# Expert slots filled from both ends, and unscaled products for two sequences, in a two-layer network on one Trainium2 core

## The chip, the cores and the metric

The kernel runs on one core of one Trainium2 chip. The core has TensorE (PE, matmuls; its weight loads are shown as PEld), VectorE (DVE), ScalarE (ACT), GpSimd (POOL, which also issues the indirect DMAs) and SyncE (SP, which issues most other DMAs). The metric is the device time of one execution in microseconds (us). A profiled execution has a span (first to last instruction) and a time of its own that is slightly longer.

## What is computed

The input is `x`, 32 sequences of 256 tokens with 256 features, and a few conditions for each sequence. Cut to its last lines, the reference is

```python
x = x + L0_attn(L0_cond(x, cond_512))             # 16 heads, two softmax attentions
x = x + L0_ffn(L0_cond2(x, cond_512))             # attention, then a mixture of experts
x = x + L1_attn(L1_cond(x, cond_512))             # kernel features of normed q and k
x = x + L1_ffn(L1_cond2(x, ids, ..., cond_64))    # conditioned norms, then butterflies
```

Two pieces matter here. The mixture of experts works on all T = 8192 tokens at once:

```python
top1 = argmax(logits); top2 = argmax(logits without top1)     # 8 experts
loc1 = cumsum(m1) - 1                     # place of a token among those that chose the expert first
loc2 = cumsum(m2) - 1 + m1.sum(0)         # second choices stand behind all first choices
m1 = m1 * (loc1 < C); m2 = m2 * (loc2 < C)                    # C = T / 4 = 2048 places
h = relu(buf[e] @ w1[e] + b1[e]);  y = (h @ w2[e] + b2[e]) * 0.8
out = t1 * y[top1, s1] + t2 * y[top2, s2]                     # t1, t2: gates, normed to sum 1
```

Which tokens an expert keeps depends on `loc` and C. In which order the kept ones are worked on does not enter the result.

The last attention of layer 1 divides q and k by their norms over the whole batch, `q / norm(q)`, `k / norm(k)`, two scalars that are known only when all sequences are done. Then it forms `exp` of a linear function of both: per sequence `exp(yT @ (rn_q * Wq' + rn_k * Wk') + bias)`, where `rn_q` and `rn_k` are the reciprocals of these norms and `Wq'`, `Wk'` are weights prepared earlier.

## The kernel before

The work stands in generator functions that yield the engine and an assumed cost of each step. `side_by_side` merges them, when the program is built, into one order for each engine, by those costs and by "join" marks; each engine then works through its list in order and waits on semaphores. A pause is written `yield None, x`, and a turn object such as `lanes_b` limits how many parts run at once. Changing one part's steps or costs can therefore move instructions of others.

There are four stages.

1. The 32 sequences go through layer 0's attentions, up to about 1583 us. The normed rows that the experts read are stored to DRAM in `h2buf`. When the first 28 sequences are done, their routing is computed beside the other work (`routed_early`): `choices_of` finds both choices, `places_of` counts (`cnt`, `cntb`) and finds places by products with a triangle (`loc`, L569 to L584), `tokens_of` turns the places into a list of tokens by products of one-hot tiles (`tps`, L626). The last 4 sequences make LATE = 8 of the NT = 64 tiles of 128 tokens.
2. Behind a branch (L1440: a second, exact pass over the sequences, which these inputs do not take) comes the routing of the late tiles, `routing` (L1503 to L1525). `ends` (L1527) finds per expert where first choices end; for each expert, first choices fill the slots from the front and second choices from the back, so the number of tokens of each kind must be known first. The late token list is added to the early one (`both` L1514), the two sides are joined (`to` L1517, L1518) and give `tok` (L1520), the token of every slot. `slots` and `gates` (L1552, L1568) compute rows and gates; the gates are transposed (L1612), copied (L1615) and stored to `gbuf` in DRAM (L1618).
3. The experts: 8 experts of CAP = 2048 slots in blocks of CBLK = 512, so 4 blocks for each. `expert_block` (L1675) gathers 4 x 128 rows by `tok` on POOL's queue (L1686), transposes them on PE (L1700) and copies them with ACT (L1703, `ehT`). The first layer is 16 matmul instructions in 8 banks (`bh` L1740), followed by ACT (`hid` L1727), the second layer 32 instructions (`by` L1757), and DVE adds the bias (`ysb` L1763) and multiplies by the gate of the slot (`gslot` L1772). POOL gathers these gates from `gbuf` (L1633, `slot_gates`) and adds the rows to the tokens in DRAM with a scatter (L1643, `add_to_tokens`). A scatter adds to memory, so each waits for the landing of the one before. `load_expert` (L1659) loads w1, w2 and b2 of an expert on SP's queue; for the second expert it waits for a small POOL memset (`behind_gathers`, L1657) behind the first gathers. Each fp32 matmul instruction shows as two records in the trace.
   Beside the experts, DVE multiplies the butterflies of the last feed-forward into a dense matrix (`butterflies` L1809, `butterfly_stage` L1786, with the loads `w_eff` and `bfw`), and shares its buffers with the experts' tiles.
4. `answer` (L1889) finishes the experts' rows of each sequence. `norms` (L2174) sums the squares (`qs`, L2184), and takes the factors `rn` on POOL (L2191), then scales and adds the weights (`mixed`, L2197, L2198). `norm_rows` (L2200) makes the row of biases `aphr` (L2208, L2212) and a scalar `phs`. `answer_out` (L2261), 32 times, is the last phase: the values and the mixed product (L317, by `project`), `exp`, the gathers of norm tables (L2227, on POOL), statistics and their power (L261, L267), modulated norms (L2246, L2248), their transposes (L297) and products (L2353), and the two dense products (L2410, L2424).

PSUM banks and SBUF buffers come from rings named "mm", "sh" and "big": `get` takes the next buffer, `back` returns it, and an instruction that writes a reused buffer waits for its former readers.

Of the kernel before, what the change touches and what calls it, by code (L numbers as in the profile page):

```python
# [14 lines left out]
F = mybir.dt.float32  # L15
# [7 lines left out]
P = 128  # L23
# [195 lines left out]
def network(ctx: ExitStack, tc: tile.TileContext, a: dict, out: bass.AP):  # L219
# [304 lines left out]
    early = cst.tile([P, 2, 2 * NHI], F, name="early")  # L524
# [35 lines left out]
    def places_of(a, b):  # L560
# [3 lines left out]
        wide = [(min(b, (n + 1) * SLAB) - n * SLAB) * NE for n in range(n1)]  # L564
        cps = yield from get("mm", "cnt", [P, 2, NSB])
# [6 lines left out]
        for n in range(n0, n1):  # L572
            yield DVE, 0.15
            nc.vector.tensor_copy(cntb[: wide[n], :, n], cps[: wide[n], :, n])
        yield back("mm")
        step = 2 if 2 * W * NE <= 512 else 1
        for k0 in range(0, 2, step):
# [3 lines left out]
            for i in range(step):  # L581
                nc.tensor.matmul(loc[:, i, :], utb, mbs[:, k0 + i, a * NE : b * NE], start=True, stop=False)
                for n in range(n1):
                    nc.tensor.matmul(  # L584
                        loc[:, i, :], cntb[: wide[n], k0 + i, n : n + 1].to_broadcast([wide[n], P]),
                        before[: wide[n], n, a * NE : b * NE], start=False, stop=(n == n1 - 1),
                    )
# [10 lines left out]
    def tokens_of(a, b, wide, into):  # L598
# [11 lines left out]
        for k, (op, at) in enumerate(((ALU.add, NE * CAP - 1), (ALU.subtract, (NE + 1) * CAP))):  # L610
# [8 lines left out]
        tps = yield from get("mm", "tps", [P, 2, 2 * NHI])  # L619
# [3 lines left out]
        def product(ol, oh, k, t, w):  # L623
            yield PE, 0.135 * w
            for i in range(w):
                nc.tensor.matmul(  # L626
                    tps[:, k, :], ol[:, i // 2, :, i % 2], oh[:, i // 2, :, :, i % 2].rearrange("p a h -> p (a h)"),
                    start=(t + i == 0), stop=(t + i == W - 1),
                )
# [3 lines left out]
        def by_place(ol, oh, o1, k, t, w, before):  # L633
            yield ACT, 0.15 + 0.125 * w
            nc.scalar.activation(oh[:, :, 1, :, :], o1, AF.Copy, scale=prow)
            yield back("sh")
            if before is not None:
# [26 lines left out]
    def routed_early(sequences):  # L664
# [8 lines left out]
        nc.vector.tensor_copy(early, got[0])  # L673
        yield back("mm")
# [803 lines left out]
    wphi, aphi = waq["aq"], abq["aq"]  # L1478
# [22 lines left out]
    cc = wD.tile([P, 2, NE], F, name="cc")  # L1501

    def routing():  # L1503
# [6 lines left out]
        both = yield from get("sh", "both", [P, 2, 2, NHI])  # L1510
        to = wD.tile([P, 2, NHI], F, name="to")
        yield "join", counted
        yield DVE, 0.75
        nc.vector.tensor_add(both.rearrange("p k a h -> p k (a h)"), got[0], early)  # L1514
        yield back("mm")
        yield DVE2, 1.0
        nc.vector.tensor_tensor(to, both[:, 1], late.unsqueeze(1).to_broadcast([P, 2, NHI]), ALU.mult)  # L1517
        nc.vector.tensor_add(to, to, both[:, 0])  # L1518
        yield DVE, 0.3
        nc.vector.scalar_tensor_tensor(tok, to[:, 0], float(P), to[:, 1], ALU.mult, ALU.add)  # L1520
        yield back("sh")
# [5 lines left out]
    def ends():  # L1527

        ps = yield from get("mm", "mm", [P, 2, NE])
        yield PE, 0.5  # L1530
        for k in range(2):
            for n in range(NSB):
                w = min(SLAB, NT - n * SLAB) * NE
                nc.tensor.matmul(
                    ps[:, k, :], cntb[:w, k, n : n + 1].to_broadcast([w, P]), e8b[:w],
                    start=(n == 0), stop=(n == NSB - 1),
                )
# [3 lines left out]
        from_ = wD.tile([P, NE], F, name="from_")  # L1541
        E3 = [P, NE, CAP // P]
        yield DVE, 1.0
        nc.vector.tensor_scalar(from_, cc[:, 1, :], -1.0, float(CAP), ALU.mult, ALU.add)
        for o, v in ((late, cc[:, 0, :]), (used, from_)):
            nc.vector.tensor_tensor(
                o.rearrange("p (e h) -> p e h", e=NE), place.unsqueeze(1).to_broadcast(E3),
                v.unsqueeze(2).to_broadcast(E3), ALU.is_ge,
            )
        nc.vector.scalar_tensor_tensor(used, late, 0.0, used, ALU.is_equal, ALU.max)  # L1550
# [17 lines left out]
    def gates():  # L1568
# [3 lines left out]
        sm_, den = column("sm_"), column("den")  # L1572
        yield DVE2, 0.7
# [9 lines left out]
        for k in range(2):  # L1583
            m = mbs[:, k, :].rearrange("p (t e) -> p t e", e=NE)
            s_ = nths[:, k, :]
            if k == 1:

                s_ = column("s1")
                yield DVE2, 0.7
# [995 lines left out]
```

## Time and profile before

| | |
|---|---|
| runs | 3622.98, 3613.11, 3611.27 us; median 3613.11 |
| profiled execution | 3614.65 us |
| its span | 3612.9 us |
| mean granted clock of PE | 0.978 |
| PE busy | 3433.1 us (95%) |
| sequences | 0 to about 1583 us |
| branch left | 1586.3 us (first work behind it: DVE 1586.27, SP 1586.30) |
| late routing, PE partly idle | 1586.3 to 1600.4 us |
| experts, PE full | 1610 to 2523 us |
| answers and norms | 2523 to 2683 us |
| last phase | 2683 to 3613 us |

The page lists for each engine its busy time and share of the span, then the span in slices, the DMA queues, the chain of work that ended last, and the groups of instructions by line. A row of the timeline gives the start and duration in us, the engine, the line, the operation, out<-in with shapes, a count, and in brackets how long the engine was idle before and what ended that. A row of windows gives for a stretch its length and the busy time of each engine in it (with the count of instructions), then the clock that PE was granted (1.00 is full speed), the mean busy share of the DMA engines, and GB/s. Busy PE is not PE at its peak: a matmul at half clock counts as busy too.

### The profile page before, as it was taken

Reading aid. Unit: us, or ns where it says so; the run is one execution under the profiler, and the core shown is the slowest. Engines: PE = TensorE matmul, PEld = TensorE weight load, DVE = VectorE, ACT = ScalarE, POOL = GpSimd, SP = SyncE. Lnnn points to the kernel's source line nnn. Section 1 sums busy time; section 2 is a strip of 40 time slices with the busy share of each in tenths; the row PEclk is TensorE's granted clock in tenths of the full one; section 3 lists DMA queues with packets and bytes.
Section 4 is the critical chain, followed back from the end, with each engine's and each line's share of the span. In section 5 each row is a group of like instructions: output and inputs, shape, how many; then the busy total and the mean of one; then the engine's idle time right before and its main releaser. Section 6 shows DMA issues by size and latency. Waiting matters only on the chain. (4 is left out here: it accounts for less than half of the span.)

```text
span 3612.9 us, 55000 instructions
## 1 busy us (share of the span) xinstructions
PE 3433.1 (95%) x21397; PEld 2522.7 (70%) x21397; DVE 2295.8 (64%) x3817; ACT 1780.4 (49%) x2751; POOL 1733.7 (48%) x1388
## 2 busy tenths in 40 slices
PE   6798999999999999959999999999989999999999
PEld 5465566666666666636666666667878888888888
DVE  7988889988888884647665620101347666666664
ACT  2677778888787877732222222223334333343332
POOL 3655756566466555226545555553123334344331
PEclk9899999999999999979999999999999999999999
DMA  3344434444444442133334333332441323233221
GB/s 86 66 95 96 92 91 105 104 97 103 94 100 99 100 96 71 56 121 107 89 91 109 106 73 52 64 54 47 161 143 39 123 97 113 80 124 101 97 97 44
DMA packets 192239, 332.67 MB, mean 92 GB/s; under 512 B 55041, under 2 KB 116673, under 8 KB 181730
## 3 DMA queue, kind: packets, MB, share of 16 engines
q0 software_dynamic: 56768, 163.68, 20.1%
q1 hardware_dynamic: 135058, 164.86, 14.6%
q8 instruction: 171, 2.80, 0.3%
q14 instruction: 98, 0.80, 0.1%
q10 hardware_dynamic: 144, 0.52, 0.0%
HBM read 204.03 MB, written 52.58 MB: 71 GB/s over the span
## 5 line engine op out<-in xcount | busy, mean ns | idle before, releaser
L1090 ACT ACTIVATE pt<-sc 128x2048 f32<-128x2048 f32 x256 | 481.5, 1881 | 122.8 <-PE sc L1081 116.1
L1727 ACT ACTIVATE hid<-bh,cols 128x512 f32<-128x512 f32 (+1 forms) x261 | 175.9, 674 | 604.5 <-PE bh L1740 603.4
L1757 PE MATMUL by<-w,hid 128*128 128x256 f32 x2048 | 452.2, 379 | 0.0
L1740 PE MATMUL bh<-ehT,w 128*128 128x512 f32 (+1 forms) x1056 | 450.8, 581 | 0.1
L1757 PEld LDWEIGHTS by<-w,hid 128*128 128x128 f32 x2048 | 387.4, 190 | 65.3 <-issue 15.8
L267 POOL TENSOR_TENSOR n<-n,negh 128x32 f32<-128x32 f32 x64 | 366.9, 5733 | 5.3
L1740 PEld LDWEIGHTS bh<-ehT,w 128*128 128x128 f32 x1056 | 200.6, 191 | 216.4 <-issue 207.5
L261 POOL TENSOR_SCALAR rstd<-mv 128x2 f32<-128x2 f32 x160 | 65.9, 412 | 583.0 <-DVE mv L367 563.1
L1643 POOL DMA_INDIRECT rrows<-ysb,row x128 | 222.6, 1739 | 253.3 <-DMA rrows<-ysb,row 138.4
L1763 DVE TENSOR_TENSOR ysb<-by,b 128x512 f32<-128x512 f32 (+1 forms) x66 | 44.5, 674 | 469.6 <-PE by L1757 431.8
L1081 PE MATMUL sc<-qT,kT 32*128 32x256 f32 x4096 | 298.7, 406 | 14.4 <-ACT pt L1090 12.6
L1063 PE MATMUL av<-pt,vaug 128*32 128x256 f32 x4096 | 276.0, 387 | 7.0 <-ACT pt L1090 6.1
L893 DVE TENSOR_TENSOR hprod<-hex,kk 128x2048 f32<-128x2048 f32 x120 | 275.9, 2320 | 0.0
L1081 PEld LDWEIGHTS sc<-qT,kT 32*128 32x128 f32 x4096 | 188.2, 187 | 102.8 <-issue 52.1
L2410 PE MATMUL dh<-zT,w_eff 128*128 128x256 f32 x1024 | 235.4, 379 | 0.6 <-DVE zT L2386 0.6
L2424 PE MATMUL do<-w_con,gT 128*128 128x256 f32 x1024 | 231.1, 379 | 0.0
L2424 PEld LDWEIGHTS do<-w_con,gT 128*128 128x128 f32 x1024 | 192.5, 190 | 24.9
L2410 PEld LDWEIGHTS dh<-zT,w_eff 128*128 128x128 f32 x1024 | 189.8, 190 | 24.3 <-DVE zT L2386 1.0
L1686 POOL DMA_INDIRECT xg<-h2buf,tok x128 | 139.9, 1093 | 137.4 <-issue 31.8
L1063 PEld LDWEIGHTS av<-pt,vaug 128*32 128x32 f32 x4096 | 107.5, 110 | 135.5 <-issue 67.6
L2400 ACT ACTIVATE gT<-dh,b_eff 128x256 f32<-128x256 f32 x256 | 106.2, 472 | 141.4 <-PE dh L2410 138.8
L267 POOL TENSOR_TENSOR rstd<-rstd,negh 128x2 f32<-128x2 f32 x160 | 164.1, 1025 | 13.3
(622 smaller groups left out, 7023.9 us busy)
## 6 DMA issues: line engine op xcount, KB each, us to landing
hprod<-hprod POOLq DMA_DIRECT2D x60, 1024.0 KB, 7.8
oT<-rden SPq DMA_DIRECT2D x64, 256.0 KB
w<-in_w SPq DMA_DIRECT2D x16, 1024.0 KB
x<-rrows SPq DMA_DIRECT2D x64, 256.0 KB
bfw<-in_upw SPq DMA_DIRECT2D x10, 1024.0 KB
bfw<-in_dnw SPq DMA_DIRECT2D x10, 1024.0 KB
xT<-in_xT SPq DMA_DIRECT2D x32, 256.0 KB
avT<-avT SPq DMA_DIRECT2D x256, 32.0 KB
```

Of the source, the lines that this page charges most:

```text
L267: nc.gpsimd.tensor_tensor(o, o, negh[:p].to_broadcast([p, n]), ALU.pow)
L893: nc.vector.tensor_tensor(pr.rearrange("p j (h d) -> p j h d", d=DH), weights(t, j0, 8)[:, 0].unsqueeze(3).to_broadcast([P, 8, H, DH]), wi ...
L1063: nc.tensor.matmul(av[32 * i : 32 * i + 32, c % 2, :], va[:, kc, HO * (4 * c + i) : HO * (4 * c + i) + 32], pt[:, i, kc, :], start=(kc == ...
L1081: nc.tensor.matmul(sc[:, i, kc, :], kT[r, m, kc * P : (kc + 1) * P], qT[r, e, m, :], start=True, stop=nm is None,)
L1090: nc.scalar.activation(pt, sc, AF.Exp, scale=1.0 / math.sqrt(DH))
L1643: nc.gpsimd.indirect_dma_start(rrows[:, :], bass.IndirectOffsetOnAxis(ap=row[:, j0 + t : j0 + t + 1], axis=0), y[:, t, :], None, compute_o ...
L1686: nc.gpsimd.indirect_dma_start(xg[t], None, h2buf[:, :], bass.IndirectOffsetOnAxis(ap=tok[:, j : j + 1], axis=0))
L1727: nc.scalar.activation(o, ps, AF.Relu, bias=bcol)
L1740: nc.tensor.matmul(ps, w["w1"][:, c, f * P : (f + 1) * P], hT[c][:, c0 : c0 + wide * P], start=(c == 0), stop=(c == 1))
L1757: nc.tensor.matmul(ps[:, t, :], hid[f // 4][:, f % 4, (t0 + t) * P : (t0 + t + 1) * P], w["w2"][:, f, :], start=(f == 0), stop=(f == 7),)
L2410: nc.tensor.matmul(ps[:, g, :], w_eff[:, c, f * P : (f + 1) * P], zT[:, c, :], start=(c == 0), stop=(c == 1))
L2424: nc.tensor.matmul(ps[:, t, :], gT[:, f, t * P : (t + 1) * P], w_con[:, f, :], start=(f == 0), stop=(f == 7))
```

## The change

There are two parts.

**Slots.** Early tokens (the first 28 sequences), first and second choices alike, now fill an expert's slots from the front, and late tokens from the back. So the early list is final when `routed_early` ends, and a new tile `etok` holds it. Blocks 0 and 1 of each expert (`ahead`, the first 1024 of 2048 slots) gather by `etok` and don't join the late routing; blocks 2 and 3 gather by `tok` as before. To place second choices behind first ones within the early tokens, `places_of` multiplies the counts of the first choice into the places of the second; the late tiles have counts of their own (`lcnt`). Both choices go into one accumulation `tps` of half the width. `ends` finds four borders per expert rather than one, `gates` adds the other side's counts to the places. The load of the first expert is split: w1 at once, w2 behind the gathers of block 0. The parts are listed in another order, with the butterflies behind the routing, and there are some pauses (8.0, 5.0, 30.0, 4.0).

```diff
+    etok = cst.tile([P, NHI], I32, name="etok")
...
-                for n in range(n1):
+                for n in range(n0, n1):
+                    w = wide[n]
+                    if k0 + i == 1:
+                        nc.tensor.matmul(
+                            loc[:, i, :].rearrange("p (t e) -> p t e", e=NE), counts[:w, 0, n : n + 1].to_broadcast([w, P]),
+                            e8b[:w].unsqueeze(1).to_broadcast([w, W, NE]), start=False, stop=False,
+                        )
...
-        for k, (op, at) in enumerate(((ALU.add, NE * CAP - 1), (ALU.subtract, (NE + 1) * CAP))):
+        op, at = (ALU.add, NE * CAP - 1) if a == 0 else (ALU.subtract, (NE + 1) * CAP)
+        for k in range(2):
...
-                    start=(t + i == 0), stop=(t + i == W - 1),
+                    start=(k == 0 and t + i == 0), stop=(k == 1 and t + i == W - 1),
...
+        nc.vector.scalar_tensor_tensor(etok, early[:, 0], float(P), early[:, 1], ALU.mult, ALU.add)
...
-        nc.vector.tensor_add(both.rearrange("p k a h -> p k (a h)"), got[0], early)
+        nc.vector.tensor_tensor(to, got[0], of_late.unsqueeze(1).to_broadcast([P, 2, NHI]), ALU.mult)
...
-        nc.vector.tensor_tensor(to, both[:, 1], late.unsqueeze(1).to_broadcast([P, 2, NHI]), ALU.mult)
-        nc.vector.tensor_add(to, to, both[:, 0])
+        nc.vector.tensor_tensor(early, early, of_early.unsqueeze(1).to_broadcast([P, 2, NHI]), ALU.mult)
+        nc.vector.tensor_add(to, to, early)
...
+        yield None, 5.0
         ps = yield from get("mm", "mm", [P, P])
         yield PE, 0.2
         nc.tensor.transpose(ps[: 2 * NT, :], g12.rearrange("p k t -> p (k t)"), ident)
...
         nc.sync.dma_start(w["w1"], a["w1"][e].rearrange("(c p) f -> p c f", p=P))
+        if e == 0:
+            yield DMA, 3.0
+            yield None, 2.0
+            yield first_half
+            yield from behind_gathers(w["w2"][:, 0, 0:1])
...
-        yield "join", routed
+        ahead = blk < (CAP - LATE * P) // CBLK
+        if not ahead:
+            yield "join", routed
...
-                xg[t], None, h2buf[:, :], bass.IndirectOffsetOnAxis(ap=tok[:, j : j + 1], axis=0)
+                xg[t], None, h2buf[:, :], bass.IndirectOffsetOnAxis(ap=(etok if ahead else tok)[:, j : j + 1], axis=0)
...
-    matrices = Part(butterflies([]))
+    matrices = Part(butterflies([routed]))
...
-            [routed, loads[0], blocks[0], loads[1], matrices, *blocks[1:], weights_part, *loads[2:], table_part, *first_parts, square_part, norm_part, rows_part]
+            [loads[0], routed, blocks[0], blocks[1], loads[1], matrices, *blocks[2:], weights_part, *loads[2:], table_part, *first_parts, square_part, brows, norm_part, rows_part, scaled_part]
```

**Last phase.** For the first two sequences, `answer_out` multiplies by `Wq'` and `Wk'` unscaled, before the norms are known, and leaves both products in PSUM. When `rn` is there, two DVE operations scale and add them. The biases become rows earlier (`bias_rows`, from unscaled ones) and are scaled with `rn`. The weights for the other 30 sequences are scaled later (`scaled_weights`), into the same tile.

```diff
+        if b < 2:
+            yield "join", phi_there
+            for n in ("aq", "ak"):
+                ps = yield from get("mm", "mm", [P, 2, D])
+                two.append(ps)
+                yield PE, 1.75
+                project(ps, yT, waq[n])
+            yield unscaled[b]
+            yield back("sh")
...
+        if b < 2:
+            rn = norm["rn"]
+            yield DVE, 1.5
+            nc.vector.scalar_tensor_tensor(ph, two[1], rn[:, 1:2], rows, ALU.mult, ALU.add)
+            nc.vector.scalar_tensor_tensor(ph, two[0], rn[:, 0:1], ph, ALU.mult, ALU.add)
+            yield back("mm")
+        else:
+            yield "join", scaled_part
...
         norm.update(tot=tot, rn=rn)
-        yield DVE, 1.2
-        mixed(waq, rn)
+        yield "join", brows
+        yield DVE, 0.7
+        nc.vector.tensor_scalar_mul(aphr, brow["aq"], rn[:, 0:1])
+        nc.vector.scalar_tensor_tensor(aphr, brow["ak"], rn[:, 1:2], aphr, ALU.mult, ALU.add)
+
+    def bias_rows():
+
+        yield "join", phi_there
+        yield "join", first_parts[4]
+        for n in ("aq", "ak"):
+            ps = yield from get("mm", "mm", TS)
+            yield PE, 0.5
+            for c in range(2):
+                nc.tensor.matmul(
+                    ps[:, 0, c * P : (c + 1) * P], abq[n][:, c : c + 1].to_broadcast([P, P]), ident, start=True, stop=True
+                )
+            yield ACT, 0.4
+            nc.scalar.copy(brow[n], ps[:, 0, :])
+            yield back("mm")
```

## The prediction

> **What bounds the kernel now.** I read the page first, then the windows where its PE digits are not 9, then the timelines of those windows, and the chain of waits for the second.
>
> ```profile
> span 3612.9 us, 55000 instructions
> PE 3433.1 (95%) x21397; PEld 2522.7 (70%) x21397; DVE 2295.8 (64%) x3817; ACT 1780.4 (49%) x2751; POOL 1733.7 (48%) x1388
> ```
>
> PE is idle for only 180 us in all. Nothing that shortens DVE, ACT or POOL work beside a busy PE can matter; what counts is where PE stands still. The windows show two such places near the diff:
>
> ```profile
> core 0: us, PE busy (x) PEld busy (x) DVE busy (x) ACT busy (x) POOL busy (x), PEclk, DMA share, GB/s
> 1580.00:1590.00 10.00, 2.69 (x16) 2.17 (x14) 2.48 (x12) 1.19 (x3) 0.00 (x0) 0.50 0.33 114
> 1590.00:1600.00 10.00, 4.44 (x34) 2.74 (x31) 7.96 (x25) 2.30 (x2) 0.00 (x0) 0.50 0.45 144
> 1600.00:1610.00 10.00, 2.43 (x8) 1.48 (x8) 9.50 (x24) 1.06 (x2) 6.29 (x8) 0.50 0.32 88
> 1610.00:1620.00 10.00, 9.92 (x22) 4.28 (x21) 1.62 (x6) 3.87 (x6) 7.57 (x8) 0.85 1.03 354
> 2690.00:2700.00 10.00, 6.79 (x29) 5.37 (x28) 8.24 (x21) 2.05 (x4) 7.87 (x8) 0.92 0.80 264
> 2700.00:2710.00 10.00, 2.24 (x9) 1.49 (x9) 8.04 (x17) 1.17 (x2) 3.19 (x5) 0.59 0.22 82
> ```
>
> From 1610 on PE is full until 2523 (eight experts, 913 us, 114 us each). The first gap is the routing of the last sequences' tokens ahead of the first expert; the second is the start of the last phase. What ends the first gap:
>
> ```profile
> 1600.14 0.29 DVE L1520 SCALAR_TENSOR_TENSOR tok<-to 128x128 int32<-128x128 f32 x1
> 1602.15 1.16 POOL L1686 DMA_INDIRECT xg<-h2buf,tok  x1 [23.53 <-DVE rf L1562]
> 1608.99 1.33 PE L1700 MATMUL mm<-ident,xg 128*128 128x128 f32 x5 [0.74 <-DMA xg<-h2buf,tok]
> 1610.40 2.07 PE L1740 MATMUL bh<-ehT,w 128*128 128x512 f32 x2
> ```
>
> POOL has waited 23.53 us for the token list; from its first gather to the first expert product pass 1610.40 − 1602.15 = 8.25 us.
>
> **Expert slots, the start.** The list `etok` is finished before the branch at L1440, and blocks 0 and 1 no longer wait for late routing. POOL can gather when the branch is left; the other engines' first work behind it is at 1586.27 (DVE) and 1586.30 (SP), so I take 1586.4. Plus 8.25, the first product is at 1594.65 rather than 1610.40: **−15.75 us**. The late one-hot and place matmuls ahead of it stay, and take 2 us from 1588.21 to 1590.9, before the first gather lands. Both kernels start the experts cold (clock 0.50 until 1613), so no gain is booked for the clock.
>
> Now w1 of expert 0 (1 MB, issued 1586.30) travels beside these gathers; before, they had the queues to themselves. At the 376 GB/s of the window 1610 to 1615 it takes 2.8 us, so the gathers lose between 0 and 2.8; they are small and interleave, so I take **+0.3**. w2 waits behind them, is issued near 1592 and is needed by the first second-layer product, at 1594.65 + 12 first-layer products, the tokens' matmuls and 4 more: about 1612.5. That is cover of some 15 us.
> The Trainium skill ("DMA: Bandwidth & Descriptors", section "Latency and other measured facts") speaks against this step: it gives an HBM access 0.2 us on average and 2 us under high load, so gathers beside a load would land up to 1.8 us later; by that the sum below would be worse by 1.5 us. No row here shows gathers of these rows landing beside a load that PE waited for.
>
> **What moves into the busy stretch.** The 16 token products (L626) stood in the gap (3.57 us at clock 0.50); now they run between first-layer products. At full clock half: **+1.8**. Gates, ends and slots grow by some twenty small DVE operations (0.15 to 0.7 us by the rows of L1514 to L1607), all beside a PE that has work; uncovered they would be about 6 us.
>
> **The backlog this leaves.** The gates are late relative to the experts. Token list at 1611.7 (second group of tokens' products at about 1610.5, then three DVE steps); gates 11.3 us as in the rows from 1600.35 to 1611.7, plus 2 for their added operations: 1625. The transposed gates are copied on DVE only behind the first butterflies (seven operations, 7.7 us by L1799 at 1.04, L1801, L1803 and L1805): 1633 to 1635. The store and its landing take 2.5 to 5.9 us (5.86 from the store at 1623.45 to the first gate gather at 1629.31). So POOL's gate gathers start near 1637, 42 us behind the first product; before, 19 us (1629.31 − 1610.40). Everything behind is ordered: scatters wait for gates, and buffers of the output rows for scatters. By the instruction orders the first thing late is a DVE butterfly operation on the bias row (second weights), which takes the eighth scatter's buffer; behind it on DVE stand three more and the evacuation of a second-layer bank, and for that bank PE waits. PE comes there at about 1699.6: 64 first-layer instructions at 0.86, 96 second-layer ones at 0.43, transposes, tokens and cold start, 105 us.
> POOL's path to that landing: 16 gate gathers, 8 token gathers and 8 scatters; for four of the scatters the landing is waited out (three are followed by another scatter, the eighth is the one needed).
>
> ```profile
> 1646.67 3.38 POOL L1633 DMA_INDIRECT gslot<-gbuf,grow  x1 [0.30 <-issue]
> 1676.78 0.95 POOL L1633 DMA_INDIRECT gslot<-gbuf,grow  x1 [0.31 <-issue]
> 1680.53 1.63 POOL L1643 DMA_INDIRECT rrows<-ysb,row  x1 [0.30 <-issue]
> 1685.41 3.98 POOL L1643 DMA_INDIRECT rrows<-ysb,row  x1 [3.25 <-DVE ysb L1772]
> ```
>
> A gate gather costs 1.25 in a quiet stretch and 1.65 on average over the 16 from 1629 to 1680.5; a token gather 1.25 to 1.65; a scatter 2.0 when others follow, 4.9 when the next is a scatter (1685.41 − 1680.53). So: low 16 × 1.25 + 8 × 1.25 + 4 × 4.7 + 4 × 2.0 = 57 us, high 16 × 1.65 + 8 × 1.5 + 4 × 4.9 + 4 × 2.0 = 66. From 1637: landing at 1694 to 1703, the bank free 4.2 later at 1698 to 1707. PE waits 0 to 7.6 (11 if the store lands late). I take **+1.0**: the low prices are those of stretches without a 1 MB load, and after has one such load there (the next butterfly weights), not two. Afterwards POOL catches up, since the later waits on the lists have 8 us or more of slack by the same walk.
>
> **Early routing** has four more matmuls on its counts; L584 shows 0.25 each, in a stretch where PE is nearly full: 0 to 1, taken **+0.3**.
>
> **The last phase.** Before, the norm factor (L2191) is followed by the scaling of the weights, the first mixed product and the row of biases. The chain of waits, however, goes another way:
>
> ```profile
> 2683.40 0.73 POOL rn L2191
> 2699.10 1.45 POOL ga L2227
> 2700.63 0.20 POOL rstd L261
> 2700.90 0.73 POOL rstd L267
> 2711.20 1.11 PE mm L297 x4
> 2712.32 3.82 PE mm L2353 x10
> ```
>
> Behind the factor POOL issues twelve table gathers (2684.32 to 2700.55, 1.35 each) before the statistics' power, though the statistics were ready at 2697.93. So the removal of scaling and product from DVE and PE shortens the chain only as far as POOL allows. In the new order ten gathers stand before it: 2 × 1.35 = −2.7. Statistics come about 10 us behind the factor, so POOL still decides. Against that, the unscaled products stand ahead of the factor's matmul (L2184) on PE: three of the four are in front, at 1.89 each (L317 at 2679.18), and the four matmuls of the bias rows, 1.06 cold, half when warm. PE waited 0.88 before L2184, which they fill first: 5.67 + 0.53 − 0.88 = 5.3 later. **+2.6**; bounds −2.7 (the factor not delayed) and +5.3 (nothing won behind it). The copies of bias rows (2 on ACT) and the weights' scaling for the other sequences (1.24 us on DVE) lie beside work.
> As to the clock, it is granted 1.00 until 2684 and 0.50 from 2685 to 2691, after 2.5 us of idle PE, and the first mixed product takes 3.75 rather than 1.9. The Trainium skill ("TensorE: Matmul & The Clock Gate", Part 1) lets the clock fall after an idle window of about 3.4 us; the shorter idle here suffices, so the measurement decides. By the page this product would have been warm and the removed work 1.9 us smaller, which changes nothing in a sum set by POOL.
>
> **Sum.** −15.75 + 0.3 + 1.8 + 1.0 + 0.3 + 2.6 = −9.75. From the profiled execution, 3614.65 (span 3612.9 and 1.75 around it): 3604.9. That execution is 1.54 above the median 3613.11 of the runs, so **3603.4**. With the best bounds (0, 1.8, 0, 0, −2.7): −16.7, 3596.5; with the worst (2.8, 1.8, 11, 1, 5.3): +6, 3619. No change can be told within 0.3%, 10.8 us: 3602.3 is the border.
>
> **Rivals.**
> A. The last phase pays at once: the products fit into idle PE and the factor isn't delayed. Then −2.7 in place of +2.6: 3598. For it: PE is idle from 2683.1 to 2685.6 and again for 9 us at 2697. Against: the order puts three products before L2184, where 1.86 of 2.00 us are busy (2680 to 2682).
> B. The backlog costs the whole middle to top of its bounds, 4 to 9 us: 3606 to 3611. For it: gate gathers of 3.38 and 1.7 us; against, the quiet ones.
> C, the slower side. POOL becomes the bound of whole experts. An expert needs 16 gate gathers at 1.65, 16 token gathers at 1.3 and 16 scatters: 47 + 2.0 × 16 = 79 us, and 2.9 more for each scatter that directly follows another; from 12 of 16 on it passes PE's 114. All 16 chained: 126, 12 more per expert; three experts until it recovers: −10.75 + 36 = +25, 3638. Against: 4 of the first 9 scatters are chained; for: the late gates bunch them, and POOL waited for scatters' landings 138 us already.
> D. It doesn't do what it says: the first gathers still wait (for late rows of `h2buf`, the same semaphores or the new list). Then the start is as before, and +2.9 of additions remain: 3616. Against: the last row was stored at 1579.42, before the branch.
>
> **How the numbers follow.** Forecast 0.52, half of it below the border (its own range 3599 to 3608); A 0.18; B 0.18; C 0.06; D 0.06. Faster: 0.26 + 0.18 = 0.44. Slower by over 0.3% only C: 0.06. Within: 0.50. Leaving out C, D and the tails of A and B, the range is 3594 to 3613.
>
> **What would show it.** First L1740 product of the experts near 1594.7, PE windows full from 1595; gate gathers starting near 1637; an idle PE of 0 to 8 us near 1700, released by DVE's evacuation; L2184 about 5 us later relative to the experts' end, and the first L2353 product 25.3 us behind the factor rather than 28. The prediction is wrong if first gathers come well after 1587, if PE waits for banks in more than one expert, or if statistics, not POOL, end last in the second gap.

## The result: 0.2% slower, and two waits of PE inside the experts

| | before | after |
|---|---|---|
| median of the runs shown together (14 each) | 3617.21 us | 3623.94 us |
| ratio, 95% interval | | 1.002, 1.001 to 1.0029 |
| profiled execution | 3614.65 us | 3622.64 us |
| its span | 3612.9 us | 3620.9 us |

The changed kernel is slower by 6.7 us, less than the 0.3% that the prediction named as the border, but outside its range, 3594 to 3613 around 3603.4. The head of the profile of after, with the span and the engines' busy time, has the same work in a longer span:

```profile
span 3620.9 us, 55086 instructions
...
PE 3434.4 (95%) x21418; PEld 2520.9 (70%) x21418; DVE 2303.0 (64%) x3841; ACT 1782.6 (49%) x2754; POOL 1723.3 (48%) x1389
```

I cut both spans at four places: the first work behind the branch, the first expert product (`bh`), the start of the last second-layer product (`by`) and the end. The numbers come from the timelines and from the first and last start of the two product lines.

| us | before | after | difference |
|---|---|---|---|
| start to branch | 1586.27 | 1579.58 | -6.7 |
| branch to first expert product | 24.13 | 10.10 | -14.0 |
| first to last expert product | 912.3 | 938.3 | +26.0 |
| last expert product to the end | 1090.2 | 1092.9 | +2.7 |

The first row is not a gain to be counted. The branch is left at 1574.99 to 1590.38 in the thirteen profiles of this study, and kernels whose difference lies wholly behind the branch differ in it. The other three rows are stable, and from here on times are taken behind the branch. There the change costs +14.7 us in these two executions, twice the difference of the medians; the rest of that gap belongs to the first row, and I come back to it.

Windows of after (start and end, length, busy time of PE, PEld, DVE, ACT, POOL, then granted clock, share of the DMA engines, GB/s) around the first gap, at the two new places, and around the second gap:

```profile
1580.00:1590.00 10.00, 4.14 (x26) 2.98 (x27) 8.24 (x29) 0.85 (x2) 7.09 (x7) 0.50 0.52 177
1590.00:1600.00 10.00, 10.00 (x22) 4.16 (x22) 3.60 (x22) 6.05 (x8) 1.42 (x6) 0.93 0.74 247
...
1690.00:1700.00 10.00, 6.21 (x22) 4.26 (x21) 7.44 (x10) 2.71 (x4) 6.17 (x5) 0.86 0.55 133
...
2100.00:2110.00 10.00, 8.53 (x42) 6.85 (x40) 0.01 (x1) 0.41 (x1) 7.87 (x8) 1.00 0.28 61
2110.00:2120.00 10.00, 0.00 (x0) 0.00 (x0) 5.26 (x7) 0.00 (x0) 4.68 (x4) 0.69 0.25 26
2120.00:2130.00 10.00, 5.60 (x17) 4.08 (x18) 0.35 (x2) 2.80 (x4) 4.70 (x4) 0.63 0.27 39
2690.00:2700.00 10.00, 5.33 (x26) 4.39 (x24) 7.33 (x20) 1.46 (x3) 6.23 (x7) 0.87 0.43 116
2700.00:2710.00 10.00, 4.50 (x12) 3.27 (x12) 7.21 (x16) 0.58 (x1) 8.13 (x9) 0.50 0.75 255
```

PE is full from 1590, twenty microseconds sooner than before: the start does what it was forecast to do. But inside the experts, where before had no idle PE at all (912.89 of 913.00 us busy from 1610 to 2523), PE stands still once near 1694 and for whole windows near 2115. The list of PE's waits of after between the first and the last expert product (line, what it waited for, us in total, times, longest) has both at its head, and behind them only 0.8 us for token gathers; the same list of before is empty.

```profile
PE bh L1805 <- ACT ehT L1768: 15.9, 1, 15.9
PE by L1823 <- DVE ysb L1829: 3.8, 1, 3.8
```

**The start.** Rows of the timeline of after:

```profile
1579.58 0.22 DVE L550 TENSOR_REDUCE tops<-L_all 128x8 f32<-128x64 f32 x1 [6.77 <-ACTq L1459]
...
1581.09 1.16 POOL L1750 DMA_INDIRECT xg<-h2buf,etok  x1 [9.05 <-DVE e L554]
...
1585.52 0.66 PE L1765 MATMUL mm<-ident,xg 128*128 128x128 f32 x2 [1.55 <-DMA xg<-h2buf,etok]
...
1589.68 7.50 PE L1805 MATMUL bh<-ehT,w 128*128 128x512 f32 x15
```

The first gather is issued 1.51 us behind the first DVE work rather than 0.13; the first expert product follows 8.59 us behind it, against 8.25 before. The other engines still begin the late routing in the meantime, and nobody waits for it.

**The first wait.** Gates and their way to POOL, then the place where PE stops, in the timeline of after:

```profile
1620.49 0.36 DVE L1662 SCALAR_TENSOR_TENSOR g<-g,den 128x64 f32<-128x64 f32 x2
...
1627.98 0.27 PE L1668 MATMUL mm<-ident,g 128*128 128x128 f32 x1
1628.29 0.29 DVE L1671 COPY g12T<-mm 128x128 f32<-128x128 f32 x1
1628.61 0.33 SPq L1674 DMA_DIRECT2D gbuf<-g12T  x1
...
1631.32 0.94 POOL L1690 DMA_INDIRECT gslot<-gbuf,grow  x1 [14.02 <-DMA gbuf<-g12T]
...
1688.34 1.84 POOL L1700 DMA_INDIRECT rrows<-ysb,row  x1 [2.94 <-issue]
...
1692.46 1.08 DVE L1865 TENSOR_TENSOR bft<-bfb,bfw 1x512 f32<-1x512 f32 x1 [3.73 <-DMA rrows<-ysb,row]
...
1695.94 0.67 DVE L1829 TENSOR_TENSOR ysb<-by,b 128x512 f32<-128x512 f32 x1
...
1696.67 3.63 PE L1823 MATMUL by<-w,hid 128*128 128x256 f32 x9 [3.79 <-DVE ysb L1829]
```

The gates are ready 31 us behind the first product, the first gate gather is issued 41.6 us behind it, POOL works without a pause for 61 us until the eighth scatter has landed, the butterfly operation on the bias row takes that scatter's buffer, and three more operations later the evacuation L1829 frees the bank. Two details differ from the forecast: the gates stand ready for 7 us before PE comes to their transposition, and the copy on DVE finds no butterflies in front of it.

**The second wait** lies 420 us further on. POOL, ACT, DVE and PE in the timeline of after:

```profile
2061.51 1.02 POOL L1750 DMA_INDIRECT xg<-h2buf,tok  x1 [9.82 <-DVE ysb L1829]
...
2110.64 1.63 POOL L1700 DMA_INDIRECT rrows<-ysb,row  x1 [0.30 <-issue]
...
2114.63 2.04 DVE L1865 TENSOR_TENSOR bft<-bfx,bfw 128x512 f32<-128x512 f32 x2 [14.62 <-DMA rrows<-ysb,row]
...
2114.80 2.36 POOL L1700 DMA_INDIRECT rrows<-ysb,row  x1 [2.53 <-DMA rrows<-ysb,row]
2119.64 1.56 POOL L1700 DMA_INDIRECT rrows<-ysb,row  x1 [2.48 <-DMA rrows<-ysb,row]
...
2123.57 2.11 ACT L1768 ACTIVATE ehT<-mm,cols 128x512 f32<-128x512 f32 x3 [23.16 <-DMA rrows<-ysb,row]
...
2124.40 2.08 PE L1805 MATMUL bh<-ehT,w 128*128 128x512 f32 x2 [15.87 <-ACT ehT L1768]
```

ACT wants to copy transposed rows into `ehT` and gets, from the shared ring, a buffer that still holds the rows of an expert's output. It is free when the scatter of 2119.64 has landed, at 2123.5 (in the program as built, the rows of that scatter and the `ehT` of 2123.57 have the same address). That scatter is the third of four in a row from 2110.64 on, each of which waits for the landing of the one before. POOL had stood idle for 9.82 us up to 2061.51 (and for 14.65 up to 2008.14): the token gather at the head of its queue waited for a buffer of its own, while the next scatters behind it, those of 2013.78 and 2069.00, had been ready for long: matched by the program's order, DVE had finished their rows near 1909 and 1946 (L1838).

Such waits and such rows of scatters are not peculiar to after. In the timeline of before POOL's token gathers wait too, up to 15.80 us, and five scatters stand in a row from 2083.31 on, the last of them here, and PE never stops:

```profile
1769.28 1.19 POOL L1686 DMA_INDIRECT xg<-h2buf,tok  x1 [15.80 <-PE mm L1700]
...
2100.09 1.56 POOL L1643 DMA_INDIRECT rrows<-ysb,row  x1 [2.53 <-DMA rrows<-ysb,row]
```

What costs time in after is where they meet an instruction that is handed one of their buffers.

**The clock.** Each wait is also paid behind it. In windows of 2 us the granted clock is 0.50 at 1698 to 1700 and 1.00 again from 1702; it falls between 2112 and 2114, 3.5 to 5.5 us after PE stopped, and is 1.00 again from 2128, 3.6 us after PE's return. The clock is at 0.50 for 3.41 and 2.98 us of PE's work behind the two waits, and half of that is lost: 1.7 and 1.5 us. The Trainium skill ("TensorE: Matmul & The Clock Gate", Part 1) says that the clock halves after an idle window of about 3.4 us and needs about as long a busy stretch to come back; these rows agree with it, 3.79 us of idle PE included. The row of before that the prediction sets against it does not: PE was idle from 2683.12, and the clock fell at 2684.83, 1.71 us later.

**Where the 26.0 us come from.** 15.87 + 3.79 are the two waits, 0.8 other idle time (20.57 in all against 0.12 before), 2.8 the clock (the cold start included, 4.1 lost in after and 1.3 before), and 2.7 more work on PE, of which the 16 token products make 2.1 (1.07 for each group of 8).

### The profile page after: what moved, and what is told of

Same layout as the page of the kernel before. It is cut to its first block, busy times and chain, and to the rows that moved or that the text cites. A ratio compares the mean times of both kernels' runs of the same rounds, so it can differ in the third digit from the quotient of the medians.

```text
span 3620.9 us, 55086 instructions
## 1 busy us (share of the span) xinstructions
PE 3434.4 (95%) x21418; PEld 2520.9 (70%) x21418; DVE 2303.0 (64%) x3841; ACT 1782.6 (49%) x2754; POOL 1723.3 (48%) x1389
## 5 line engine op out<-in xcount | busy, mean ns | idle before, releaser
L1805 PE MATMUL bh<-ehT,w 128*128 128x512 f32 (+1 forms) x1056 | 451.7, 581 | 15.9 <-ACT ehT L1768 15.9
L1700 POOL DMA_INDIRECT rrows<-ysb,row x128 | 217.2, 1697 | 244.4 <-DMA rrows<-ysb,row 151.8
L1829 DVE TENSOR_TENSOR ysb<-by,b 128x512 f32<-128x512 f32 (+1 forms) x66 | 44.4, 673 | 446.5 <-PE by L1823 404.3
L2509 PEld LDWEIGHTS dh<-zT,w_eff 128*128 128x128 f32 x1024 | 189.7, 190 | 24.5 <-DVE zT L2485 1.0
L267 POOL TENSOR_TENSOR rstd<-rstd,negh 128x2 f32<-128x2 f32 x160 | 162.2, 1014 | 13.3
L261 POOL TENSOR_SCALAR n<-n 128x32 f32<-128x32 f32 x64 | 53.9, 842 | 238.7 <-DVE n L958 237.6
```

The lines of the kernel that those rows point to most:

```text
L267: nc.gpsimd.tensor_tensor(o, o, negh[:p].to_broadcast([p, n]), ALU.pow)
L1700: nc.gpsimd.indirect_dma_start(rrows[:, :], bass.IndirectOffsetOnAxis(ap=row[:, j0 + t : j0 + t + 1], axis=0), y[:, t, :], None, compute_o ...
L1805: nc.tensor.matmul(ps, w["w1"][:, c, f * P : (f + 1) * P], hT[c][:, c0 : c0 + wide * P], start=(c == 0), stop=(c == 1))
L2509: nc.tensor.matmul(ps[:, g, :], w_eff[:, c, f * P : (f + 1) * P], zT[:, c, :], start=(c == 0), stop=(c == 1))
```

## Experiments

Every kernel was run beside the kernel before on the same chip. The short diffs are against the changed kernel unless they say otherwise. The table gives, for the profiled execution, the stretch from first to last expert product, PE's idle time inside it, the stretch from there to the end, and all behind the branch against before (2026.6 us).

| kernel | experts | idle | rest | behind branch | ratio to before, interval |
|---|---|---|---|---|---|
| before | 912.3 | 0.1 | 1090.2 | 0 | |
| after | 938.3 | 20.6 | 1092.9 | +14.7 | 1.002, 1.001 to 1.0029 |
| e1 slots alone | 937.7 | 19.0 | 1090.7 | +11.9 | 1.0024, 1.0011 to 1.0038 |
| e2 last phase alone | 912.0 | 0.0 | 1092.7 | +2.3 | 1.0006, 0.9992 to 1.0019 |
| e3 without the pause of 30 | 927.9 | 9.8 | 1090.9 | +2.3 | 1.0005, 0.9993 to 1.0018 |
| e4 butterflies behind gates | 930.1 | 9.8 | 1090.7 | +4.3 | 0.9994, 0.9977 to 1.0011 |
| e5 without the first 8 scatters | 948.1 | 26.8 | 1096.6 | +28.2 | single run |
| e6 three more buffers | 921.8 | 5.3 | 1096.4 | +1.7 | single run |
| e7 costs nearer to the rows | 931.7 | 11.3 | 1092.8 | +7.9 | single run |
| e8, e9 without the pause of 5 | 915.2, 914.3 | 0.1, 0.1 | 1093.0, 1091.6 | -8.3, -10.6 | 0.9959, 0.9944 to 0.9974 (e9) |
| e10 slots alone, without the pause of 5 | 914.4 | 0.1 | 1088.8 | -13.3 | 0.9955, 0.9939 to 0.9971 |
| e11 without six scatters | 930.5 | 10.4 | 1093.3 | +7.2 | single run |

### Which part makes the waits (e1, e2)

e1 has the slots of after and the last phase of before; e2 the reverse. In the list of parts, the order of e1 is

```diff
-            [loads[0], routed, blocks[0], blocks[1], loads[1], matrices, *blocks[2:], weights_part, *loads[2:], table_part, *first_parts, square_part, brows, norm_part, rows_part, scaled_part]
+            [loads[0], routed, blocks[0], blocks[1], loads[1], matrices, *blocks[2:], weights_part, *loads[2:], table_part, *first_parts, square_part, norm_part, rows_part]
```

> The slots part alone; the last phase is as before. Theory 1 (the slots win 14 us at the start, since the first expert product now comes 10.1 us behind the branch rather than 24.1, and lose about 26 us in the experts, by idle PE of 3.8 us near 1693 and 15.9 us near 2108, their cold clocks and 2 us of token products): PE idle of about 4 and 16 us in the experts as in the changed kernel, ratio to before 1.001 to 1.002, some 2.7 us under the changed kernel. Rival (the last phase's part is what costs): no idle PE over 2 us in the experts and a ratio under 0.997.

> The part on the last phase alone; slots as before. Theory 1: experts without idle PE, first dense product of the last phase about 25 us behind the norm factor rather than 28, the factor about 3.4 us later behind the experts' end, in all 2 to 3 us longer than before (ratio 1.0005 to 1.001). Rival (it pays at once): 2 to 5 us shorter.

The list of PE's waits of e1 inside the experts has both waits of after at nearly the same size:

```profile
PE bh L1804 <- ACT ehT L1767: 14.9, 1, 14.9
PE by L1822 <- DVE ysb L1828: 4.1, 1, 4.1
```

e2 has none, and its rest is 2.5 us longer than that of before, in line with e1 against after (2.2) and e9 against e10 (2.8). So the slots make the waits, and the last phase costs 2 to 3 us by itself in the profiles; in the times of e2 that can't be told from nothing. (In e5 and e6 the rest is some 3.5 us longer still than in after; why is open.)

### What is late (e3, e4, e7)

e3 takes away the pause in the middle of the butterflies, e4 lets the butterflies begin behind the gates, e7 gives the planner costs nearer to the rows of the trace.

```diff
-        yield None, 30.0
         ps = yield from get("mm", "mm", [P, 8])
```
```diff
             yield "join", p
+        for p in rest:
+            yield "join", p
         xb = yield from get("big", "bfb", [1, FF])
```
```diff
-        yield POOL, 1.1 * QT_
+        yield POOL, 1.27 * QT_
...
-            yield POOL, 1.6
+            yield POOL, 1.95
...
-            yield None, 3.0
+            yield None, 2.6
```

> The changed kernel without the pause of 30 between the first and the second half of the butterflies. Theory 1a (the second half, moved behind by the pause, takes buffers of the common ring while the scatters are late, and that makes the idle PE near 2108): the 15.9 us fall to under 3, the time by 14 to 18 us (ratio to before about 0.998). Rival 1b (the scatters are still late from the gates' late start, whatever the butterflies do): 10 us or more of idle PE stay there.

> The changed kernel with the butterflies started behind the gates rather than beside them, so that the copy of the transposed gates doesn't wait behind seven butterfly operations. Theory 1: the gate gathers start some 8 us sooner behind the first expert product (35 rather than 42), and the idle PE of 3.8 us near 1693 is gone. Rival 1b: the idle PE near 2108 goes too, or falls by half. Theory 1a: that one isn't changed by this edit except by what the merged order happens to do.

> The changed kernel, planned with the measured times of POOL's indirect DMAs (1.27 rather than 1.1 for a gather, 1.95 for the issue of a scatter rather than 1.6, and 2.6 until it has landed). Theory 1c (the order is planned with a POOL that is too quick, so gathers stand too early and scatters bunch): idle PE in the experts falls from 20.6 to under 8. Rival (the plan's costs don't matter): 15 or more.

None of them met its expectation in full. In e3 the wait for `ehT` is gone, but two waits for a bank remain, at 1693 and 2101, as its list of PE's waits in the experts says:

```profile
PE by L1823 <- DVE ysb L1829: 9.6, 2, 5.7
```

In e4 the gate gathers start 42.4 us behind the first product, no sooner than in after: the late one is PE's transposition of the gates (1632.26, 38.6 behind), which stands behind first-layer products in PE's order, and not a butterfly. That refuted my reason for the lateness. Its list of waits has other entries, 6.1 us for token gathers at 1697 to 1703 and 3.6 for a bank at 2450. In e7 the idle time is spread over many small waits, 11.3 us in all. In all three the first gate gather stays as late as in after (41.9, 42.4 and 43.6 us behind the first product), and yet the second wait shrinks or moves. That speaks against a lateness carried over 500 us, but all three edits also change the order of the rest.

### Where the second wait is made (e5, e6, e11)

e5 leaves out the first 8 scatters with the order of every engine unchanged otherwise, so that POOL's backlog at the start is gone. The eight tiles are not added to the tokens.

```diff
+            if j0 >= 2 * QT_:
+                nc.gpsimd.indirect_dma_start(
-            nc.gpsimd.indirect_dma_start(
```

> The changed kernel, its order planned as it is, without the eight scatters of the first two blocks of expert 0 (their rows are not added to the tokens). POOL's queue is shorter by 8 scatters, 1.9 to 4.9 us each, before the place where PE waited for 3.8 us. Theory 1 (the first wait is POOL's queue since the late gates): the idle PE near 1693 is gone. Rival 1b (what is late there stays late until 2108): the 15.9 us fall by 8 or more. Rival 1c (each of the two is a matter of its own place in the order): the wait of 13 to 16 us near 2108 stays.

The wait near 1693 went, as the walk of POOL's queue demands. The second wait stayed, in the timeline of PE:

```profile
2129.33 2.08 PE L1806 MATMUL bh<-ehT,w 128*128 128x512 f32 x2 [14.84 <-ACT ehT L1769]
```

So the second wait is not the first backlog still on its way. (e5 as a whole is slower; the last section says what else happened in it.)

e6 gives the shared ring three more buffers, and the planner a slightly different order with them:

```diff
-    ring(pb, "sh", 20, [P, 2, D])
+    ring(pb, "sh", 23, [P, 2, D])
```

> The changed kernel with 23 buffers rather than 20 in the common ring. Theory 1c (gathers and butterflies stand in front of scatters and wait for buffers, and the scatters behind them free buffers late): idle PE in the experts falls from 20.6 to under 6 us. Rival (POOL simply has too much to do, buffers or not): 15 us or more stay.

Its list of PE's waits inside the experts:

```profile
PE bh L1805 <- ACT ehT L1768: 2.5, 1, 2.5
PE mm L1765 <- DMA xg<-h2buf,tok: 2.4, 2, 1.4
```

At the place of the 15.9 us nothing is left: the windows from 2100 to 2130 are full. The 2.5 us for `ehT` stand at 2458, those for token gathers at 1713. That fits a buffer that was short, but the order changed as well. e11 keeps the order of all engines and leaves out six scatters shortly ahead of the four that bunched; their tiles are not added.

```diff
+            issued.append(j0 + t)
+            if not 51 < len(issued) <= 57:
+                nc.gpsimd.indirect_dma_start(
-            nc.gpsimd.indirect_dma_start(
```

> The changed kernel in its order on every engine, but without six scatters (the 51st to 56th that it issues, 2069 to 2104 us in its profile), so those six tiles of expert rows are not added to the tokens. Theory (the wait near 2108 is made by POOL's queue: the scatter that uses the buffer which the ehT copy takes is issued late behind token gathers and chained scatters): that scatter is issued about 15 us sooner, and the PE wait of 15.9 us near 2108 falls under 3 us, while the first wait (3.8 us near 1693), which lies 350 us earlier, stays between 2 and 6. Rival (the wait near 2108 comes from something that these scatters do not touch: the butterflies on DVE or ACT, or the gathers' own waits for buffers): 8 us or more stay near 2108. Six scatters' POOL time as such is worth nothing on PE's path, so the stretch from the first expert product to the last should be about 920 to 926 us by the theory and 932 or more by the rival (938.6 in the changed kernel).

The wait fell to 6.4 us, between the two bounds, and the stretch of 930.5 us is in neither range. The rows of POOL and ACT in the timeline of e11 show why:

```profile
2089.02 0.94 POOL L1753 DMA_INDIRECT xg<-h2buf,etok  x1 [11.50 <-DVE bfx L1874]
...
2095.79 1.10 POOL L1753 DMA_INDIRECT xg<-h2buf,etok  x1 [4.58 <-PE bh L1808]
...
2104.05 1.62 POOL L1703 DMA_INDIRECT rrows<-ysb,row  x1 [0.30 <-issue]
...
2117.05 2.11 ACT L1771 ACTIVATE ehT<-mm,cols 128x512 f32<-128x512 f32 x3 [13.72 <-issue]
```

The first of the four scatters is issued 1.5 us behind ACT's preceding `ehT` copy (2102.57), in after 11.0 behind it (2110.64 against 2099.64): 9.5 us sooner, and PE's wait is 9.4 us shorter. The same distance is 10.0 us in e1 (2116.86 against 2106.82) and 9.9 in e5 (2115.51 against 2105.60), with waits of 14.9 and 14.8. So in all four kernels PE's wait is 4.8 to 5.0 us more than this distance: it follows the place of these scatters in time one to one. They came only 9.5 and not 15 us sooner because the token gathers in front of them now waited 16 us for buffers of their own. So the direct cause is shown: a copy that is handed a buffer, and the place of the scatter that frees it. That the gathers' waits up to 2008 and 2061 made this place late in after is read off POOL's queue; no run took those waits away alone.

### The short pause ahead of the gates' transposition (e8, e9, e10)

If PE's transposition is what is late, the pause that the change put ahead of it is the term to take away:

```diff
             yield back("sh")
-        yield None, 5.0
         ps = yield from get("mm", "mm", [P, P])
```

> The changed kernel without the pause of 5.0 ahead of the transposition of the gates. Theory 1 (the gates are ready on DVE at 31 us behind the first expert product, but PE comes to their transposition only at 38, so all gate gathers are late by 7): the transposition moves up in PE's order by 16 first-layer products at the most; either it comes at 31 to 33, gate gathers start at 35 and the first wait of 3.8 falls under 1, or it comes before the gates are ready and PE waits there for some us. Rival: the first wait stays at 3 to 5 though the gate gathers start sooner.

> The changed kernel without the pause of 5.0, timed. Theory 1 (with the gates transposed earlier the merged order leaves no PE idle in the experts): again under 0.5 us of idle PE there, the stretch from the branch to the last expert product about 926 us rather than 948.7 (changed) and 936.7 (before); from the branch to the end 2020 us rather than 2043 and 2028. The time is that plus the first phase, 1575 to 1590 us: ratio to before 0.995 to 0.998. Rival (the one profile was luck): idle of 4 us or more in the experts, ratio 0.999 or more.

> The slots part alone, without the pause of 5.0; the last phase as before. Theory 1 (the last phase's part costs 2 to 3 us whatever the experts do): experts as in the run beside it, and 2 to 3 us shorter from the last expert product to the end (1090 rather than 1092.5), ratio to before 0.994 to 0.998. Rival (it costs nothing or pays once the experts end without a stall): 0 to 3 us longer than the run beside it.

In the timeline of e8 the gates are ready no sooner than in after (32 us behind the first product, which is at 1586.8; 31 in after), but the steps behind them follow sooner:

```profile
1619.06 0.36 DVE L1662 SCALAR_TENSOR_TENSOR g<-g,den 128x64 f32<-128x64 f32 x2
...
1621.41 0.27 PE L1667 MATMUL mm<-ident,g 128*128 128x128 f32 x1
...
1624.34 1.27 POOL L1689 DMA_INDIRECT gslot<-gbuf,grow  x1 [8.46 <-DMA gbuf<-g12T]
```

The first gate gather is 37.5 us behind the first product, 4.1 sooner than in after (35 had been expected), and both waits are gone. Its windows at the two places are full at full clock:

```profile
1690.00:1700.00 10.00, 10.00 (x52) 8.54 (x51) 9.86 (x12) 1.53 (x3) 6.10 (x5) 1.00 0.74 197
...
2110.00:2120.00 10.00, 10.00 (x26) 4.45 (x26) 8.51 (x11) 3.82 (x7) 8.20 (x6) 1.00 0.13 13
```

e9 is the same kernel timed: 3600.47 us against 3616.66, faster than before by 0.41%. e10, with the old last phase, gave 3598.01 us; the two can't be told apart by their times, though e10's profile is 2.8 us shorter behind the experts. How much of the second wait's end is due to earlier gates and how much to the order is not separated: without the pause POOL's order differs in many places all through the experts.

**First phase, open.** Behind the branch e9 is 10.6 us and e10 13.3 us shorter than before, and after 14.7 longer; the medians say 16.2 and 18.7 shorter and 6.7 longer, each 5 to 8 us better. In e1, e3 and e4 the medians are better by 2.6 to 4.7 us too, in e2, with before's slots, by 0.8. With before's slots the branch was left at 1586.27 and 1590.31 (before, e2), with the new ones at 1574.99 to 1590.38, mean 1580.9 of eleven profiles. But e8 and e9 are one and the same program, and left it at 1576.64 and 1581.67. That may be a gain of some 7 us in the first phase or chance; the difference is there by 1474 us already, where all these programs have the same order. No run separates the two.

## Why the prediction was wrong

**What bounds the kernel, and the start: right.** Forecast −15.75 + 0.3 behind the branch, measured −14.0. The missing 1.4 us are in one place: the first gather is issued 1.51 and not 0.13 us behind the first work. The prediction's own rows of before had such a stretch: the token list is ready at 1600.43 and the first gather issued at 1602.15, 1.7 us later, and the sum left it out. What POOL does in it is open; in after the trace names DVE's operation L554. From gather to first product it is 8.59 against the forecast 8.55 (8.25 plus 0.3), so the 1 MB load beside the gathers cost the 0.3 that was taken, of bounds 0 to 2.8. The Trainium skill's figure for an access under high load ("DMA: Bandwidth & Descriptors", section "Latency and other measured facts"), which the prediction weighed, allowed 1.8 us more by an estimate; this trace shows 0.34 in all. Rival D (the first gathers still wait) is refuted by the same rows.

**Token products and early routing.** +1.8 forecast, 2.1 measured. The four matmuls of early routing cost nothing: the stretch from the early to the late use of L550 is 105.0 to 105.8 us in kernels with the new slots, 105.3 before.

**The last phase: the size right, in part by luck.** +2.6 forecast, +2.7 measured. From the last expert product to the factor +3.4 (forecast +5.3), from the factor's end to the first dense product 24.98 against 27.98 us, −3.0 (forecast −2.7), and 2.3 more behind it, which the prediction had not and which wasn't traced. So the two parts that were priced make +0.4, and the untraced one brings the sum to the forecast. POOL still ends last, with ten gathers between the factor and the power, in the timeline of after:

```profile
2692.05 0.73 POOL L2259 TENSOR_TENSOR rn<-tot,negh 128x2 f32<-128x2 f32 x1 [63.16 <-DVE tot L2256]
...
2706.78 0.19 POOL L261 TENSOR_SCALAR rstd<-mv 128x2 f32<-128x2 f32 x1
```

Rival A, which had the last phase pay 2.7 us, is out. The sum's terms without the backlog, −10.75, agree with what e9 shows behind the branch, −10.6, in a kernel without waits. Part of that is luck: in e9 the start is 1.4 us worse than forecast and the stretch behind the experts 1.2 better.

**The backlog: the mechanism right, its size too small.** The place, the releaser, the length of POOL's work (61 us, forecast 57 to 66), the start of the gate gathers (41.6 us behind the first product, forecast 42) and PE's arrival (103, forecast 105) came as the prediction walked them. That the start of the gate gathers was met is partly luck: the prediction had the copy of the gates late behind butterflies, and it was PE's transposition that was late. The wait was 3.8 and not 1.0, inside the bounds 0 to 7.6: the low prices for POOL were taken where the middle held. With 1.7 us of lost clock, for which the term had no price, it cost 5.5; this alone is rival B's case.

**The step that failed** is the sentence "Afterwards POOL catches up, since the later waits on the lists have 8 us or more of slack by the same walk." The walk covered some 150 us from the first product; the experts last 938. POOL had indeed caught up: at 1726 and 1770 its scatters waited for rows of DVE, 9.9 us in all, and at 1812 a token gather 13.1 us for ACT. But 420 us behind the first wait a copy of `ehT` was handed a buffer whose scatter landed only at 2123.5, the third of four in a row, and PE waited 15.9 us, with its clock 17.4, which no term of the sum covered. e5 shows that it is not the first backlog, e11 with after, e1 and e5 that it follows the scatters' place; e6 fits a buffer that was short. That the planner had put token gathers ahead of ready scatters, and that these waited from 1993 and 2052 on, is the likely reason for the late place; before has such waits as well, without a cost. The change reached that place through the planner, which set the order of all eight experts anew when parts, costs and pauses changed at the start. I counted the instructions that the order moved near the edit and did not walk the rest. Rival C named the right engine, but POOL was not busy for whole experts: its 24.5 us of waiting for buffers up to 2008 and 2061 were time in which the next scatters were ready.

## What to carry to other kernels

Where a planner lays out the order, a change at the start rewrites it everywhere: walk each queue to the end of the stage before a stall is called local. A wait of a queue's head while ready work stands behind it is a place to look, but not yet a cost: before has such waits and loses nothing by them. A buffer ring that links two engines turns a late store into a wait of an engine that has nothing to do with it; look which buffer an instruction takes, not only which data it reads. When an early start leaves a later step on the critical chain, try the pauses on that chain first: here one assumed pause of 5 us decided between 0.2% slower and 0.4% faster, though earlier gates and changed order are not separated in that.

## What the runs showed of the hardware

In e5, with scatters gone, POOL issued 24 indirect gathers in a row from 1627 to 1657, and PE crept: from 1645 to 1660 its second-layer instructions, 0.38 us long at full clock, started 1.4, 2.1 or 2.8 us apart. The profile names no wait but "issue", 11.8 us in all. Rows of its timeline:

```profile
1647.91 0.38 PE L1824 MATMUL by<-w,hid 128*128 128x256 f32 x1 [1.05 <-issue]
...
1650.73 0.58 PE L1824 MATMUL by<-w,hid 128*128 128x256 f32 x1 [2.45 <-issue]
...
1652.14 0.79 PE L1824 MATMUL by<-w,hid 128*128 128x256 f32 x1 [0.82 <-issue]
```

The queues that carry instructions moved nothing in that stretch. The cause is open. The other surprise was the first phase: with the same order of instructions it ended up to 15 us apart from one kernel to the next, and 5.0 us apart in two runs of one program (e8 and e9).
